# Graph layer on gathered columns: list tiles for 32-row groups, multiplied on column tiles, in place of early projection of the last rows

## The chip, the core and the metric

The kernel runs on one core of a Trainium2 chip. A core has five engines that run side by side and meet at semaphores: TensorE (PE, matmuls, with weight loads shown apart as PEld), VectorE (DVE), ScalarE (ACT), GpSimd (POOL) and SyncE (SP, which here only issues transfers). SBUF is its working memory, PSUM holds matmul results in banks, and 16 DMA engines carry data between SBUF and the memory outside (DRAM). The metric is the device time of the program in microseconds (us); lower is better.

## The reference

With x of 8 x 4096 x 256, adj of 4096 x 4096 and W of 256 x 256, all float32:

```python
HW = jnp.einsum('bnf,fo->bno', H, W)
A_norm = jax.nn.relu((A + A.T) * 0.5)
D = jnp.sum(A_norm, axis=1)
d_inv_sqrt = jnp.where(D > 0, D_safe ** (-0.5), 0.0)
DAD = d_inv_sqrt[:, None] * A_norm * d_inv_sqrt[None, :]
L_norm = jnp.eye(N) - DAD
out = jax.nn.relu(jnp.einsum('nm,bmo->bno', L_norm, HW))
result = layernorm(x + out)     # over the last axis
```

adj is sparse: 0.42% of the symmetrised matrix is not zero, and the entries are denser at low row and column numbers. The matrix is one for all eight batches, so one row of `g` (x W scaled by r, for all batches) has 8 x 256 = 2048 numbers, 8 KB.

## The kernel before, in words

The 4096 rows form 32 blocks of 128 (`NB`), and stage 1 walks squares of 512 rows (`NS` = 8 squares a side, `A` = 4 blocks each).

**Stage 1** (L191 to L308). For each pair of squares (i, j) with j >= i both adj squares are loaded (1 MB each, on SP's queue). `symmetrise` (L207) transposes on PE, adds on DVE (L215), halves and clips on ACT (L216), sums stretches of 128 columns into `part` (L217, DVE) and stores the result to `a_dram` from ACT's queue. When a row of squares is complete, `degrees` (L227) forms the degrees `e` and, with a power on POOL, `r`. `form(m, known)` (L238) projects block m: load of x (1 MB, SP), 16 transposes, 64 issued matmuls with W, then a copy on ACT and a store to `g_dram`. Where r of the block is known, ACT scales by it in the copy (L266). The last eight blocks (`HOLD`) are projected in the first row of squares, when no r is known: they are kept in SBUF (`held`), and `release` (L274) scales and stores them after the last degree. A `credit` of one projection for each pair of squares spreads the work.

**Lists.** A block of rows i needs only the columns in which one of its 128 rows has an entry. `places(s)` (L106) turns `part` into a mask for four blocks, and with two matmuls and a scan on DVE gives each used column a place; `make_list(i)` (L146) turns places into lists of row numbers: `hot` (L149) and three smaller comparisons and products on DVE, then 32 short matmuls (L169). A list tile holds 128 places. `CAP` fixes how many tiles a block has: 29 for the first, 9 for the last, 390 in all. Places that no column uses point to a row of zeros (row N of `a_dram` and `g_dram`).

**Stage 2** (L347 to L395). For each list tile POOL issues two indirect transfers: 128 pieces of 512 bytes of the symmetrised matrix (`ga`, L358), and 128 rows of g (`gg`, L365, 1 MB), each into one of ten buffers. PE multiplies them into four PSUM banks of 512 columns (L384); an f32 matmul is issued twice, so a tile is 8 matmuls. When all tiles of a block are in, `finish` (L311) subtracts from e times the block's own g (`gself`, loaded on SP's queue), applies r and relu on ACT, adds x and normalises on DVE, with a power on POOL (L334), and stores the output from ACT's queue.

The order on each engine is not the text's: a planner orders instructions by priority and readiness and sets the semaphores. If a block's list overflowed, a flag would start a full product (L403), which is not run with these inputs.

Of the kernel before, what the change touches and what calls it, by code (L numbers as in the profile page):

```python
# [8 lines left out]
F32 = mybir.dt.float32  # L9
# [7 lines left out]
CAP = [29, 21, 18, 17, 16, 15, 14, 13, 13, 13, 12, 12, 12, 11, 11, 11, 11] + [10] * 6 + [9] * 9  # L17
# [3 lines left out]
def kernel(  # L21
# [21 lines left out]
    nc = tc.nc  # L43
# [9 lines left out]
    HOLD = 8  # L53
    EPS = 1e-5

# [8 lines left out]
    part = const.tile([P, NB, NB], F32, name="part")  # L64
# [15 lines left out]
    lists = {}  # L80
    tmax = max(CAP)
# [19 lines left out]
    carry = const.tile([P, A, NB], F32, name="carry")  # L101
    nc.vector.memset(carry, 1.0)
    nc.vector.memset(carry[:, :, 0:1], 0.0)
    over = const.tile([P, NB], F32, name="over")

    def places(s):  # L106

        mask = ipool.tile([P, A, NB], BF16, tag="mask", name=f"mask_{s}")
        nc.vector.tensor_scalar(
            mask, part[:, :, s * A : (s + 1) * A].rearrange("p m i -> p i m"), 0.0, None, ALU.is_gt  # L110
        )
        pc = psum.tile([P, 2, A * NB], F32, tag="ix", name=f"count_{s}", bufs=2)
        mflat = mask.rearrange("p i m -> p (i m)")
        nc.tensor.matmul(pc[:, 0, :], lhsT=lower, rhs=mflat, start=True, stop=True)
        nc.tensor.matmul(pc[:, 1, :], lhsT=ones, rhs=mflat, start=True, stop=True)
        incl = ipool.tile([P, A * NB], F32, tag="incl", name=f"incl_{s}")
        nc.vector.tensor_tensor_scan(
            incl, carry.rearrange("p i m -> p (i m)"), pc[:, 1, :], 0.0, ALU.mult, ALU.add
        )
        for k in range(A):  # L120
            i = s * A + k
            nc.vector.tensor_scalar(
                over[:, i : i + 1],
                incl[:, (k + 1) * NB - 1 : (k + 1) * NB],
                float(CAP[i] * P),
                None,
                ALU.is_gt,
            )
        pos = ipool.tile([P, A * NB], F32, tag="pos", name=f"pos_{s}")
        nc.vector.tensor_sub(pos, incl, pc[:, 1, :])  # L130
        nc.vector.tensor_add(pos, pos, pc[:, 0, :])
        ip = ipool.tile([P, A * NB], I32, tag="ip", name=f"ip_{s}")
        nc.vector.tensor_copy(ip, pos)
        quot = ipool.tile([P, A * NB], I32, tag="quot", name=f"quot_{s}")
        nc.vector.tensor_single_scalar(quot, ip, 7, ALU.arith_shift_right)
        rem = ipool.tile([P, A * NB], I32, tag="rem", name=f"rem_{s}")
        nc.vector.tensor_single_scalar(rem, ip, P - 1, ALU.bitwise_and)

        at = ipool.tile([P, 2, A, NB], F32, tag="at", name=f"at_{s}")
        aq = at[:, 0].rearrange("p i m -> p (i m)")  # L140
        nc.vector.scalar_tensor_tensor(aq, quot, 1.0, mflat, ALU.add, ALU.mult)
        nc.vector.tensor_scalar(aq, aq, -1.0, None, ALU.add)
        nc.vector.tensor_copy(at[:, 1].rearrange("p i m -> p (i m)"), rem)
        return at

    def make_list(i, at):  # L146
        k, t = i % A, CAP[i]
        hot = ipool.tile([P, NB, P], BF16, tag="hot", name=f"hot_{i}")
# [13 lines left out]
        val = ipool.tile([P, NB, 2, tmax], BF16, tag="val", name=f"val_{i}")  # L162
# [28 lines left out]
    with (  # L191
        tc.tile_pool(name="adj", bufs=4) as apool,
        tc.tile_pool(name="hold", bufs=HOLD) as hpool,
# [13 lines left out]
        def symmetrise(i, j, tij, tji):  # L207
            sym = spool.tile([P, A, S], F32, tag="sym", name=f"sym_{i}_{j}")
            for a in range(A):
# [8 lines left out]
                part[:, i * A : (i + 1) * A, j * A : (j + 1) * A],  # L218
                sym.rearrange("p a (c q) -> p a c q", q=P),
# [16 lines left out]
        held = {}  # L236

        def form(m, known):  # L238

            xin = xpool.tile([P, B, F], F32, tag="xin", name=f"xin_{m}")  # L240
            nc.sync.dma_start(xin, x[:, m * P : (m + 1) * P, :].rearrange("b p f -> p b f"))
            xt = xpool.tile([P, B, FC, P], F32, tag="xt", name=f"xt_{m}", bufs=1)
# [6 lines left out]
            if known:  # L249
                g = xpool.tile([P, G], F32, tag="g", name=f"gt_{m}")  # L250
            else:
                g = hpool.tile([P, G], F32, tag="held", name=f"held_{m}")
            for b in range(0, B, 2):
# [10 lines left out]
                to = g[:, b * FO : (b + 2) * FO]  # L264
                if known:
                    nc.scalar.mul(to, pg, r[:, m : m + 1])  # L266
                else:
                    nc.scalar.copy(to, pg)
            if known:
                nc.scalar.dma_start(g_dram[m * P : (m + 1) * P, :], g)  # L270
            else:
                held[m] = g

        def release(m):  # L274
            g = held.pop(m)
            nc.scalar.mul(g, g, r[:, m : m + 1])
            nc.scalar.dma_start(g_dram[m * P : (m + 1) * P, :], g)


        known, early = [], list(range(NB - HOLD, NB))  # L280
        credit = 0.0
        for i in range(NS):
            for j in range(i, NS):
# [5 lines left out]
                credit += 1.0 if j > i else 0.5  # L289
                while credit >= 1.0 and (known or early):  # L290
                    if known:
                        form(known.pop(0), True)
                    else:
                        form(early.pop(0), False)
                    credit -= 1.0
# [161 lines left out]
```

## Time and profile before

| What | us |
|---|---|
| Median of three runs (1978.11 to 1985.22) | 1980.13 |
| The profiled execution's own time | 1980.13 |
| Its span, first to last instruction | 1978.2 |
| PE busy | 1819.9 |
| POOL busy | 918.9 |
| DVE busy | 887.4 |
| ACT busy | 348.1 |
| First `gg` gather starts at | 568.4 |
| Multiplication of list tiles on PE, from and to | 578.5 to 1957.8 |

Transfers moved 738 MB, 434.6 MB of it by POOL's gathers. In the profile's lines a group is: source line, engine, operation, output <- inputs, shape, count, then busy time in us and mean in ns, then the idle time of the engine just before these instructions and what ended it. In a listing in order of time, the two first numbers are start and length in us. In a list of stretches, each engine's busy time and instruction count follow the stretch, then the clock that TensorE was granted, the busy share of the DMA engines and GB/s. The chain of waits is what ended last, followed back.

### The profile page before, as it was taken

The numbers are of one execution on the slowest core, as the hardware profiler recorded it, in microseconds if no ns is written. First come the engines' busy times: TensorE is split into PE (matmuls) and PEld (weight loads), VectorE is DVE, ScalarE is ACT, GpSimd is POOL, SyncE is SP. The second block draws the span as 40 slices with busy tenths as digits, with TensorE's granted clock in tenths as the row PEclk, the third lists the DMA queues.
The fourth block names the chain that finished last, engine by engine and source line by source line (L and its number), as shares of the span: only waits on it lengthen the run. The fifth ranks groups of instructions, "written<-read, shape, count | busy, mean of one in ns | idle before, by whom it ended". The sixth has DMA issues, their size and how long they took to land.

```text
span 1978.2 us, 18260 instructions
## 1 busy us (share of the span) xinstructions
PE 1819.9 (92%) x6720; PEld 1006.8 (51%) x6720; DVE 887.4 (45%) x1679; ACT 348.1 (18%) x361; POOL 918.9 (46%) x830
## 2 busy tenths in 40 slices
PE   6988686879669999999999999999999999999995
PEld 5877575768544444444444444444444444444442
DVE  4778898755300102432226424523733733343334
ACT  3654443545620000000000000000000000000000
POOL 0000000000045655676558766865766865666662
PEclk8999897899889999999999999999999999999998
DMA  9998999999979999999998999899899999999994
GB/s 345 384 372 328 349 369 337 353 397 382 400 278 409 387 357 369 342 378 380 381 383 317 411 409 389 338 411 413 313 401 411 368 407 411 410 412 412 413 410 191
DMA packets 245726, 738.08 MB, mean 373 GB/s; under 512 B 17136, under 2 KB 115744, under 8 KB 187520
## 3 DMA queue, kind: packets, MB, share of 16 engines
q0 software_dynamic: 68640, 434.55, 55.3%
q1 hardware_dynamic: 104960, 167.78, 23.8%
q10 hardware_dynamic: 72032, 134.51, 17.7%
q8 instruction: 56, 0.92, 0.2%
q14 instruction: 38, 0.31, 0.0%
HBM read 602.54 MB, written 134.24 MB: 372 GB/s over the span
## 4 chain that ended last, share of the span: by engine, by line
PE 68%; DMA 13%; DVE 11%; issue 4%; ACT 3%; POOL 1%; SPq 0%; ACTq 0%; POOLq 0%; DVEq 0%
PE py L384 54%; PE pg L257 8%; DMA gg<-g_dram,gi 7%; PE tr L212 3%; DVE hot L149 3%; DMA a_dram<-sym 2%; DVE sym L215 2%; DMA adj<-in_adj_dram 2%; PE xtr L247 2%; DVE part L217 1%; ACT sym L216 1%; DMA xin<-in_x_dram 1%; PE pl L169 1%; DVE stats L331 1%; DVE y L326 1%
## 5 line engine op out<-in xcount | busy, mean ns | idle before, releaser
L384 PE MATMUL py<-gg,ga 128*128 128x512 f32 x3120 | 1363.6, 596 | 18.4 <-issue 16.0
L384 PEld LDWEIGHTS py<-gg,ga 128*128 128x128 f32 x3120 | 585.7, 190 | 726.6 <-issue 717.7
L358 POOL DMA_INDIRECT ga<-a_dram,ai x390 | 425.0, 1090 | 269.8 <-PE py L384 145.2
L365 POOL DMA_INDIRECT gg<-g_dram,gi x390 | 414.9, 1064 | 226.4 <-DMA gg<-g_dram,gi 109.7
L325 ACT ACTIVATE y<-y,r 128x2048 f32<-128x2048 f32 x32 | 64.1, 2002 | 1332.8 <-DVE y L317 1213.5
L257 PE MATMUL pg<-w_sb,xt 128*128 128x256 f32 x1024 | 247.6, 398 | 38.2 <-ACT xt L248 38.1
L317 DVE SCALAR_TENSOR_TENSOR y<-gself,e,py 128x512 f32<-128x512 f32 x128 | 95.1, 747 | 408.0 <-PE py L384 398.6
L234 POOL TENSOR_TENSOR r<-e,neg_half 128x4 f32<-128x4 f32 x8 | 8.1, 1011 | 510.3 <-DVE e L233 510.3
L257 PEld LDWEIGHTS pg<-w_sb,xt 128*128 128x128 f32 x1024 | 198.9, 199 | 76.3 <-ACT xt L248 48.5
L215 DVE TENSOR_TENSOR sym<-tr,adj 128x512 f32<-128x512 f32 x256 | 158.3, 683 | 115.4 <-PE tr L212 105.3
L212 PE MATMUL tr<-ident,adj 128*128 128x128 f32 x1024 | 132.1, 289 | 58.5 <-DVE sym L215 34.6
L185 DVE TENSOR_SCALAR ai<-low 128x9 uint32<-128x9 f32 (+11 forms) x32 | 6.5, 204 | 369.1 <-DMA ga<-a_dram,ai 369.1
L149 DVE TENSOR_TENSOR hot<-iota_q,at 128x4096 bf16<-128x4096 f32 x32 | 141.4, 4420 | 63.9 <-PE pl L169 48.9
L212 PEld LDWEIGHTS tr<-ident,adj 128*128 128x128 f32 x1024 | 123.7, 150 | 65.9 <-DVE sym L215 40.3
L217 DVE TENSOR_REDUCE part<-sym 128x16 f32<-128x2048 f32 x64 | 144.7, 2278 | 13.1 <-ACT sym L216 13.1
L216 ACT ACTIVATE sym<-sym 128x2048 f32<-128x2048 f32 x64 | 122.5, 1914 | 111.2 <-DVE sym L215 110.6
L336 DVE TENSOR_SCALAR y<-y,mv,rstd 128x256 f32<-128x256 f32 x256 | 87.2, 412 | 43.4 <-POOL rstd L334 43.4
L331 DVE BATCH_NORM_STATS2 stats<-y 128x6 f32<-128x256 f32 x256 | 99.3, 400 | 0.9
L326 DVE TENSOR_TENSOR y<-y,xr 128x2048 f32<-128x2048 f32 x32 | 73.4, 2293 | 56.0 <-ACT y L325 45.7
L334 POOL TENSOR_TENSOR rstd<-rstd,neg_half 128x8 f32<-128x8 f32 x32 | 69.5, 2173 | 42.2 <-DVE rstd L333 41.6
L248 ACT COPY xt<-xtr 128x512 f32<-128x512 f32 x128 | 69.8, 582 | 62.1 <-PE xtr L247 50.9
L247 PE MATMUL xtr<-ident,xin 128*128 128x128 f32 x512 | 72.5, 297 | 7.6 <-DVE sym L215 7.2
(50 smaller groups left out, 398.4 us busy)
## 6 DMA issues: line engine op xcount, KB each, us to landing
adj<-in_adj_dram SPq DMA_DIRECT2D x64, 1024.0 KB
a_dram<-sym ACTq DMA_DIRECT2D x64, 1024.0 KB
xin<-in_x_dram SPq DMA_DIRECT2D x32, 1024.0 KB
gself<-g_dram SPq DMA_DIRECT2D x32, 1024.0 KB
xr<-in_x_dram SPq DMA_DIRECT2D x32, 1024.0 KB
out_dram<-y ACTq DMA_DIRECT2D x32, 1024.0 KB
g_dram<-gt ACTq DMA_DIRECT2D x24, 1024.0 KB
g_dram<-held ACTq DMA_DIRECT2D x8, 1024.0 KB
```

Of the source, the lines that this page charges most:

```text
L149: nc.vector.tensor_tensor(hot, iota_q.unsqueeze(1).to_broadcast([P, NB, P]), at[:, 1, k, :].unsqueeze(2).to_broadcast([P, NB, P]), ALU.is_ ...
L212: nc.tensor.transpose(pt[:, c * P : (c + 1) * P], tji[:, c, a * P : (a + 1) * P], ident)
L215: nc.vector.tensor_add(sym[:, a, :], pt, tij[:, a, :])
L216: nc.scalar.activation(sym, sym, AF.Relu, scale=0.5)
L217: nc.vector.tensor_reduce(part[:, i * A : (i + 1) * A, j * A : (j + 1) * A], sym.rearrange("p a (c q) -> p a c q", q=P), AX.X, ALU.add,)
L247: nc.tensor.transpose(pt[:, k, c, :], xin[:, b + k, c * P : (c + 1) * P], ident)
L257: nc.tensor.matmul(pg[:, k * FO : (k + 1) * FO], lhsT=xt[:, b + k, c, :], rhs=w_sb[:, c, :], start=(c == 0), stop=(c == FC - 1),)
L317: nc.vector.scalar_tensor_tensor(yf[:, c * S : (c + 1) * S], gself[:, c * S : (c + 1) * S], e[:, i : i + 1], py[c], ALU.mult, ALU.subtract,)
L331: nc.vector.bn_stats(stats[:, b, :], y[:, b, :])
L358: nc.gpsimd.indirect_dma_start(out=at, out_offset=None, in_=a_rows, in_offset=bass.IndirectOffsetOnAxis(ap=ai[:, t : t + 1], axis=0),)
L365: nc.gpsimd.indirect_dma_start(out=gt, out_offset=None, in_=g_dram, in_offset=bass.IndirectOffsetOnAxis(ap=gi[:, t : t + 1], axis=0),)
L384: nc.tensor.matmul(py[c], lhsT=at, rhs=gt[:, c * S : (c + 1) * S], start=(t == 0), stop=(t == CAP[i] - 1),)
```

## The change

- **Two kinds of list tiles.** `part` now keeps sums of 32 columns. `places` finds, for each block, the columns used by exactly one of its four groups of 32 rows. Those get places in tiles of that group (`SINGLE` tiles for each group); all other columns, and what does not fit there, get places in common tiles (`MULTI`). That is 122 common tiles and 71 x 4 group tiles, 406 in all for 390.
- **Column tiles.** A common tile is multiplied as before. Four group tiles, one of each group, form a step: each is multiplied with only its 32 columns of `ga`, into 32 partitions of the same PSUM bank. So 122 + 71 = 193 steps take the place of 390.
- **Unused places are not fetched.** The `gg` gather has a bounds check and leaves out places that point to row N; the buffers (a ring of 14, `ga` 18) are cleared once.
- **Order of gathers.** In place of gathering block i + 1 after block i, after each step as many tiles are gathered as it used, 14 ahead.
- **Projection.** No block is projected early: `project` runs only after its r is known, the four blocks of a row of squares beside the next row, the last four after the first lists. `held`, `release` and the credit are gone. `adj` has five buffers for four, `xt` two for one.
- **`finish`** loads the block's own g into y itself in place of a tile `gself`. `hot` and `val` have one buffer for two.

```diff
-CAP = [29, 21, 18, 17, 16, 15, 14, 13, 13, 13, 12, 12, 12, 11, 11, 11, 11] + [10] * 6 + [9] * 9
+MULTI = [22, 9, 7, 6, 5, 4, 4, 5, 3, 4, 4, 4, 3, 3, 3, 3, 3] + [2] * 15
+SINGLE = [2, 3, 3, 3, 3, 3, 3, 2, 3, 2, 2, 2, 2, 2, 2, 2, 2] + [2] * 15
...
+    def prefix(mask, n, reset, name):
+        tot = psum.tile([P, n], F32, tag="ix", name=f"tot_{name}", bufs=2)
+        nc.tensor.matmul(tot, lhsT=ones, rhs=mask, start=True, stop=True)
+        low = psum.tile([P, n], F32, tag="ix", name=f"low_{name}", bufs=2)
+        nc.tensor.matmul(low, lhsT=lower, rhs=mask, start=True, stop=True)
+        incl = ipool.tile([P, n], F32, tag=f"incl{n}", name=f"incl_{name}", bufs=1)
+        nc.vector.tensor_tensor_scan(incl, reset, tot, 0.0, ALU.mult, ALU.add)
+        pos = ipool.tile([P, n], F32, tag=f"pos{n}", name=f"pos_{name}", bufs=1)
+        nc.vector.tensor_sub(pos, incl, tot)
+        nc.vector.tensor_add(pos, pos, low)
+        return pos, incl
...
+        cnt = ipool.tile([P, A, NB], F32, tag="cnt", name=f"cnt_{s}", bufs=1)
+        nc.vector.tensor_reduce(cnt, used.rearrange("p k c m -> p k m c"), AX.X, ALU.add)
+        one = ipool.tile([P, A, NB], BF16, tag="one", name=f"one_{s}", bufs=1)
+        nc.vector.tensor_scalar(one, cnt, 1.0, None, ALU.is_equal)
+        nc.vector.tensor_tensor(
+            used, used, one.unsqueeze(2).to_broadcast([P, A, K, NB]), ALU.mult
+        )
+        pos, _ = prefix(
+            used.rearrange("p k c m -> p (k c m)"),
+            A * K * NB,
+            carry.rearrange("p k c m -> p (k c m)"),
+            f"s{s}",
+        )
...
-        held = {}
-        def form(m, known):
+        def project(m):
...
-            if known:
-                nc.scalar.dma_start(g_dram[m * P : (m + 1) * P, :], g)
-            else:
-                held[m] = g
-        def release(m):
-            g = held.pop(m)
-            nc.scalar.mul(g, g, r[:, m : m + 1])
             nc.scalar.dma_start(g_dram[m * P : (m + 1) * P, :], g)
...
+                for _ in range(-(-len(todo) // (NS - j))):
+                    project(todo.pop(0))
             degrees(i)
+            todo += range(i * A, (i + 1) * A)
...
+        nc.sync.dma_start(yf, g_dram[i * P : (i + 1) * P, :])
         for c in range(G // S):
             nc.vector.scalar_tensor_tensor(
                 yf[:, c * S : (c + 1) * S],
-                gself[:, c * S : (c + 1) * S],
+                yf[:, c * S : (c + 1) * S],
...
+        ring = [gath.tile([P, G], F32, tag=f"g{k}", name=f"g{k}", bufs=1) for k in range(RING)]
+        for gt in ring:
+            nc.vector.memset(gt, 0.0)
...
+            gt = ring[n % RING]
+            nc.gpsimd.indirect_dma_start(
+                out=gt,
+                out_offset=None,
+                in_=g_dram,
+                in_offset=bass.IndirectOffsetOnAxis(ap=gi[:, t : t + 1], axis=0),
+                bounds_check=N - 1,
+                oob_is_err=False,
+            )
...
+                    for d, (at, gt) in enumerate(tiles):
+                        ds = slice(d * Q, (d + 1) * Q)
+                        nc.tensor.matmul(
+                            py[c][ds, :],
+                            lhsT=at[:, ds],
+                            rhs=gt[:, cols],
+                            start=first,
+                            stop=last,
+                            skip_group_check=True,
+                        )
+            for _ in ts:
+                gather(n)
+                n += 1
+            if last:
+                finish(i, py, ypool, stat)
```

## The prediction

> **What bounds the kernel now.** I read the page first for the stages. Its slices change at 562 us: ahead of it all engines work, behind it PE is full.
>
> ```profile
> PE   6988686879669999999999999999999999999995
> DMA  9998999999979999999998999899899999999994
> L384 PE MATMUL py<-gg,ga 128*128 128x512 f32 x3120 | 1363.6, 596 | 18.4 <-issue 16.0
> L358 POOL DMA_INDIRECT ga<-a_dram,ai x390 | 425.0, 1090 | 269.8 <-PE py L384 145.2
> L365 POOL DMA_INDIRECT gg<-g_dram,gi x390 | 414.9, 1064 | 226.4 <-DMA gg<-g_dram,gi 109.7
> ```
>
> PE and the DMA engines are both near full. Busy shares do not say which has room, so I cut the span in stretches (length, PE, PEld, DVE, ACT, POOL busy, clock, DMA share, GB/s):
>
> ```profile
> 0.00:519.00 519.00, 416.25 (x2720) 366.96 (x2721) 385.25 (x468) 255.96 (x296) 8.43 (x17) 0.92 0.98 363
> ...
> 1800.00:1900.00 100.00, 99.07 (x231) 43.38 (x231) 38.34 (x95) 8.01 (x4) 63.53 (x59) 1.00 1.03 412
> ```
>
> Stage 1 moves 363 GB/s with DMA at 0.98 and PE at 80%: transfers set its pace. Late in stage 2 the rate is 412 to 413 for 200 us; I take 413 GB/s as the ceiling. The chain there alternates between the two limits:
>
> ```profile
> 1652.25 55.05 PE py L384 x128
> ...
> 1731.57 13.90 DMA gg<-g_dram,gi
> 1745.73 14.47 DMA gg<-g_dram,gi
> ...
> 1905.84 51.96 PE py L384 x120
> ```
>
> From the first line, 128 matmuls in 55.05 us are 0.430 us each and 3.44 us for a list tile (8, since an f32 matmul is issued twice). 390 tiles are 1342 us of PE, plus some 37 us of list matmuls and gaps: PE works from 578.5 to 1957.8, 1379 us. The second and third show how close DMA is: a gather waits until the fourth one before it has landed (14 us), so only four tiles are in flight. Then POOL, in order of time:
>
> ```profile
> 1114.31 0.95 POOL L365 DMA_INDIRECT gg<-g_dram,gi  x1 [0.30 <-issue]
> 1115.56 0.96 POOL L358 DMA_INDIRECT ga<-a_dram,ai  x1 [0.30 <-DMA ga<-a_dram,ai]
> 1116.83 0.95 POOL L365 DMA_INDIRECT gg<-g_dram,gi  x1 [0.30 <-issue]
> ...
> 1227.28 4.72 POOL L365 DMA_INDIRECT gg<-g_dram,gi  x1 [0.31 <-issue]
> 1232.15 5.85 POOL L334 TENSOR_TENSOR rstd<-rstd,neg_half 128x8 f32<-128x8 f32 x1
> ```
>
> Unhindered, a tile costs POOL 2.51 us (two gathers of 0.95 and two gaps of 0.30). At 1227 a gather took five times as long: DVE worked on `hot` just then:
>
> ```profile
> 1226.80 4.39 DVE L149 TENSOR_TENSOR hot<-iota_q,at 128x4096 bf16<-128x4096 f32 x1
> ```
>
> **What the Trainium skill says.** (1) "TensorE: Matmul & The Clock Gate", Part 3, Measured speedup vs the span model: three column tiles at N=512 gave 2.38 times. No run here shows one. (2) "TensorEngine Tiling (Array Packing)", Key Properties: changing the tiling mode drains TensorE; that is two changes a block, nothing against 33 us. (3) "SBUF — State Buffer", Who interferes with whom: a DVE instruction with two SBUF inputs contends with a GpSimd instruction that reads SBUF. The trace agrees: 4.72 for 0.95 us. (4) "DMA: Bandwidth & Descriptors", The descriptor swizzle: in a transfer over 128 partitions, the DMA engine follows from the partition, engines 0 to 7 writing partitions 0 to 63. The trace does not name engines.
>
> **The change, part by part.** Counted from the reference's inputs, 45,244 (block, column) rows are used. No region overflows (the tightest has 379 of 384 places), so the full path stays off.
>
> PE. Of 406 tiles 122 stay full: 122 x 3.44 = 420 us. The other 284 go in 71 steps of four. If the four do not overlap a step is 4 x 3.44 = 13.8 us; if they overlap fully, 3.44. Each f32 matmul is two passes of one column tile[...] I expect the second pass of one beside the first of the next: half of 13.8, 6.9 us. 71 x 6.9 = 490. PE then needs 910 us for 1342 and has room whatever lies between 3.44 and about 12 us. With gaps PE is granted less clock: 0.78 in the stretch 562 to 600, where it waits for gathers. 910/0.78 is 1167, still below DMA.
>
> DMA. All bytes together fall: 45,244 x 8 KB = 371 MB for 409, and 16 tiles more add 1 MB. But places fill from partition 0 and the unused ones are the last of a region, so they sit in the upper partitions. If engines follow partitions, the busiest engine fetches 3,115 rows; before, each had 390 x 8 = 3,120. Its bytes are 25.5 MB of g, 1.7 of a, and 6.3 of the block's own g, x and output (32 x 3 x 65,536): 33.5 MB at 413/16 = 25.8 GB/s, 1297 us, for 1296 before. The saving in bytes buys no time. If engines shared the rest, it would be 1206 us; I take 1297.
>
> POOL. 406 x 2.51 = 1019 us. `pow` 32 x (1.67 + 0.19) = 60. Each list locks POOL for `hot` and the three short operations, 5.4 us, of which some 0.6 is gap anyway: 26 lists lie in stage 2, 26 x 4.8 = 125. The residual add (2.29 us) costs some 1.7: 32 x 1.7 = 54. `places` grows from 128 to 512 elements, from about 3 to 12 us by DVE's rows of 128 elements (0.22 to 0.42); six lie in stage 2, perhaps 3 us each against POOL: 18. Sum 1276. On DVE itself the 9 us more each are covered, since it is busy 39% late in stage 2; so is the wait for list matmuls that a single `hot` and `val` buffer brings (the next list on DVE waits for PE's 32 short ones, 2 to 3 us). Uncovered, they are 54 and 26 x 3 = 78 us. A bounds check on a gather has no row: below, it may save up to 13% of 0.95 us where rows are skipped (-0.1), above, I bound it by half a gather (+0.5). I take 0.
>
> So DMA (1297) and POOL (1276) bind together, with only four tiles between them. A lock of 5 us is covered as long as the four tiles in flight (11 us) last; POOL wins back 3.2 - 2.5 us a tile. Before, with POOL at 80% of the DMA time, five late blocks took 161.6 us for 159.5 of transfers, 1.3% over. With POOL at 98% I expect a third of its lock time to show: (125 + 54) x a quarter to a third, 45 us; between 0 and 179. Sum 1342 us. The ring of 14 and the 18 `ga` buffers cost and bring nothing, since four in flight is the limit.
>
> Stage 1. Up to the last degree 24 projections lie beside the symmetrised blocks: 134.2 MB + 24 x 2.1 = 184.5 MB at 363 GB/s, 508 us. Then eight projections in PE's order, 8.66 us from one to the next (544.96 to 553.62): 577 us, for 562 before: +15. It is +4 if the four known ones are pulled ahead, +40 if the first row without projections leaves DMA idle. The eight scalings of held tiles (2 us each on ACT) go. The 14 memsets of the ring (2.3 us each at most, by the 2048-element add) lie on DVE beside the last projections, where it is idle (0.00 busy at 562 to 600); uncovered, they cost 32 us. An extra `adj` and `xt` buffer I cost at nothing, as transfers set the pace.
>
> `finish`. g now lands in y itself, so its load waits for the output of two blocks before (two y buffers). On SP nothing but the next x row queues behind it. Pow to output to load is about 6 + 10 + 11 us, and two blocks are 66: hidden; if not, DVE's subtraction, PE's banks and then the gathers are late.
>
> Sum: first g gather 568.4 + 15 = 583; 1342 to the last landing; 5 us of latency and 5 for the last step on PE; 21 from PE's end to the span's end, as before (1957.2 to 1978.2). 1956, and 2 us around the span as in the profiled execution (1980.13, which is also the median): **1958 us**, 1% faster.
>
> **Rivals.**
> - *Bytes saved count in full.* If engines share the load, DMA needs 1206 and POOL's 1276 binds, with 25 us of coupling: 583 + 1301 + 31 + 2 = 1917 us. For it: 38 MB less. Against it: the skill's partition rule.
> - *POOL becomes the bound, slower than before.* One mechanism: the bounds-checked gather costs more on POOL. With +0.35 us, 1276 + 142 = 1418 us; 583 + 1418 + 31 + 2 = 2034. It ends slower than before from about +0.22 us (406 x 0.22 = 89, and 583 + 1276 + 89 + 33 = 1981). For it: POOL has no room left, and every g gather carries the check; against it: no row shows a check, and skipped rows leave less to issue.
> - *The column tiles do not overlap.* PE needs 420 + 71 x 13.8 + 37 = 1437 us from 593 on: 593 + 1437 + 21 = 2051; with weight loads exposed (284 x 8 x 0.05 to 0.19 us) up to 2200. It decides from 12.9 us a step. For it: nothing in the trace shows overlap; against it: the skill's 2.38.
> - *The transfers were hidden anyway* is the forecast itself: PE halves and time hardly moves.
>
> **How the numbers follow.** Forecast 45% (own range 1930 to 1995: coupling 0 to 80 us, stage 1 +4 to +30); full saving 12%; dearer POOL 23%; no overlap 20%. Under 1900 lie some 4%, above 2070 some 14%. Within 0.5% (1970 to 1990), what a measurement here can tell from no change, falls a quarter of the forecast and a little of the POOL case, 14%; faster 42% (29 + 12 + 1), slower 44%.
>
> **What would show it.** The spacing of a column step: 6.9 us right, 13.8 wrong. PE idle for some 40% of stage 2, waiting for gg. GB/s lower, near 385, at a DMA share still near 1. POOL's median gather still 0.95, its waits for landings short. First g gather near 583. Wrong would be: a stage 2 at 413 GB/s (bytes do count), gathers of 1.2 us, or a stage 1 past 610.

## The result, and the profile after

The changed kernel takes 2031.84 us (median of four, 2027.29 to 2039.49) where the kernel before takes 1982.68: 1.0251 times as long, interval 1.0204 to 1.0298. The forecast was 1958 and faster, with an own range of 1930 to 1995; the time lies above that range, on the other side of no change. The profiled execution has a span of 2033.9 us.

First the page of the changed kernel: busy tenths in 40 slices of 51 us, then the groups that answer to those shown of before (busy us, mean ns, idle time just before and what ended it).

```profile
PE   4586878889978999979769989776768866557554
DMA  9999899999759999999997999998999998898892
L445 PE MATMUL py<-g,ga 128*128 128x512 f32 x976 | 493.9, 660 | 162.5 <-DVE y L350 131.9
L451 PE MATMUL py<-g,ga 128*32 128x512 f32 x2272 | 554.6, 599 | 17.4 <-issue 12.3
L416 POOL DMA_INDIRECT g<-g_dram,gi x406 | 474.4, 1168 | 192.5 <-issue 106.9
L407 POOL DMA_INDIRECT ga<-a_dram,ai x406 | 437.8, 1078 | 188.7 <-issue 110.7
```

PE is no longer full behind slice 12, as forecast, and it empties towards the end (5, 5, 7, 5, 5, 4). But the first line of matmuls waited 131.9 us for `y L350`, the subtraction in `finish`. That is not a wait for gathers, and the forecast's sum has nothing for it. And DMA has its lowest slices (7, 5), the last one apart, at 510 to 610 us, at the end of stage 1. So I took two stretches (length, PE, PEld, DVE, ACT, POOL busy, clock, DMA share, GB/s). After the change:

```profile
500.00:600.00 100.00, 96.50 (x547) 86.11 (x545) 16.07 (x21) 54.91 (x86) 2.02 (x2) 1.00 0.68 232
...
1700.00:1800.00 100.00, 61.30 (x230) 20.78 (x225) 30.48 (x83) 6.00 (x3) 62.48 (x59) 0.80 0.89 328
```

And before the change:

```profile
500.00:600.00 100.00, 68.81 (x284) 50.74 (x285) 10.00 (x13) 42.18 (x50) 26.09 (x27) 0.85 0.87 339
```

At 500 to 600 us the changed kernel is bound by PE (96.5) on projections while DMA is at 0.68; the kernel before is already in stage 2 for the last 30 us of it. At 1700 to 1800 us nothing is full: PE 61, POOL 62, DMA 0.89 at 328 GB/s, where before it was 413. Something serial holds them all. The list of waits (total, times, longest, in us) names it:

```profile
DVE y L350 <- DMA y<-g_dram: 332.1, 18, 33.6
...
POOL rstd L367 <- DVE rstd L366: 139.4, 11, 24.1
PE py L445 <- DVE y L350: 131.9, 8, 25.2
```

DVE's subtraction waits for the load of the block's own g into y, PE waits for the subtraction (it frees PSUM banks), and POOL waits in its power for DVE's statistics. (The chain of waits of this page is of no use: it breaks off 22 us before the end, at the last subtraction.) How late the load is, and why, is read from the listing in order of time over two blocks, of which only the lines that matter stand here (SPq and ACTq are instructions that issue a transfer from that engine's queue):

```profile
1689.61 2.72 DVE L350 SCALAR_TENSOR_TENSOR y<-y,e,py 128x512 f32<-128x512 f32 x4 [33.18 <-DMA y<-g_dram]
1700.17 2.67 DVE L369 TENSOR_SCALAR y<-y,mv,rstd 128x256 f32<-128x256 f32 x8
1700.41 1.82 POOL L367 TENSOR_TENSOR rstd<-rstd,neg_half 128x8 f32<-128x8 f32 x1 [15.20 <-DVE rstd L366]
1702.93 0.38 ACTq L377 DMA_DIRECT2D out_dram<-y  x1
1709.01 0.34 SPq L348 DMA_DIRECT2D y<-g_dram  x1
1718.31 2.72 DVE L350 SCALAR_TENSOR_TENSOR y<-y,e,py 128x512 f32<-128x512 f32 x4 [15.31 <-DMA y<-g_dram]
1728.86 2.68 DVE L369 TENSOR_SCALAR y<-y,mv,rstd 128x256 f32<-128x256 f32 x8
1731.63 0.38 ACTq L377 DMA_DIRECT2D out_dram<-y  x1
1755.29 0.34 SPq L348 DMA_DIRECT2D y<-g_dram  x1
1764.72 2.72 DVE L350 SCALAR_TENSOR_TENSOR y<-y,e,py 128x512 f32<-128x512 f32 x4 [32.99 <-DMA y<-g_dram]
```

This is a loop. Call the block of the first line k. The normalisation 10.6 us after it (L369) is not block k's: by the order of instructions it is that of block k-1, which the planner put behind block k's statistics. Then comes the output of k-1, and only when it has landed may y of block k+1 be loaded into the same buffer (6.1 us after the issue the first time, 23.7 us the second; in SP's own list of waits, these loads stand behind the output in 24 waits, 612 us in all). 9.3 us later the load has landed, and the subtraction of block k+1 starts. So one block, not two, goes round the loop at a time: 28.7 us, then 46.4 us, and so on in turn, 37.5 us a block where before it was 30.9. The quick landing falls just behind a pause of POOL (it had waited 15.2 us for its power, and sent its next gather only at 1702.30), the slow one amid gathers.

In the kernel before, the listing of DVE has the other order: subtraction (L317), the end of the statistics (L333), the normalisation (L336), and only then the subtraction of the next block:

```profile
1128.92 2.05 DVE L317 SCALAR_TENSOR_TENSOR y<-gself,e,py 128x512 f32<-128x512 f32 x3
1138.73 0.17 DVE L333 TENSOR_SCALAR rstd<-mv 128x8 f32<-128x8 f32 x1
1152.20 2.67 DVE L336 TENSOR_SCALAR y<-y,mv,rstd 128x256 f32<-128x256 f32 x8
1173.31 0.75 DVE L317 SCALAR_TENSOR_TENSOR y<-gself,e,py 128x512 f32<-128x512 f32 x1 [17.88 <-PE py L384]
```

By the order of instructions it is so in all 32 blocks before. In the changed kernel the normalisation is late for the first time in the seventh block, and from the twelfth block to the thirtieth it always stands behind the next block's statistics.

### The profile page after: what moved, and what is told of

The parts are those of the page before. It is cut to its first block, busy times and chain, and to the rows that moved or that the text cites. A ratio compares the mean times of both kernels' runs of the same rounds, so it can differ in the third digit from the quotient of the medians.

```text
span 2033.9 us, 19384 instructions
## 1 busy us (share of the span) xinstructions
PE 1529.4 (75%) x6862; PEld 785.6 (39%) x6864; DVE 982.5 (48%) x1853; ACT 337.0 (17%) x353; POOL 983.3 (48%) x1054
## 5 line engine op out<-in xcount | busy, mean ns | idle before, releaser
L445 PE MATMUL py<-g,ga 128*128 128x512 f32 x976 | 493.9, 660 | 162.5 <-DVE y L350 131.9
L451 PE MATMUL py<-g,ga 128*32 128x512 f32 x2272 | 554.6, 599 | 17.4 <-issue 12.3
L416 POOL DMA_INDIRECT g<-g_dram,gi x406 | 474.4, 1168 | 192.5 <-issue 106.9
L445 PEld LDWEIGHTS py<-g,ga 128*128 128x128 f32 x976 | 200.8, 212 | 460.3 <-issue 307.6
L350 DVE SCALAR_TENSOR_TENSOR y<-y,e,py 128x512 f32<-128x512 f32 x128 | 88.4, 744 | 482.5 <-DMA y<-g_dram 332.1
L451 PEld LDWEIGHTS py<-g,ga 128*32 128x32 f32 x2272 | 151.7, 110 | 398.0 <-issue 394.0
L209 DVE TENSOR_TENSOR hot<-iota_q,at 128x4096 bf16<-128x4096 f32 x32 | 141.5, 4421 | 66.0 <-PE pl L229 23.7
L276 DVE TENSOR_REDUCE part<-sym 128x64 f32<-128x2048 f32 x64 | 144.7, 2277 | 6.9 <-ACT sym L275 6.8
L229 PE MATMUL pl<-val,hot 128*128 128x20 bf16 (+10 forms) x1024 | 40.6, 175 | 114.0 <-DVE low L239 57.6
L369 DVE TENSOR_SCALAR y<-y,mv,rstd 128x256 f32<-128x256 f32 x256 | 86.1, 409 | 44.9 <-POOL rstd L367 44.9
L317 ACT ACTIVATE gt<-pg,r 128x512 f32<-128x512 f32 x128 | 87.9, 690 | 112.3 <-PE pg L310 110.2
L229 PEld LDWEIGHTS <-hot 128*128 128x128 bf16 x1024 | 38.3, 97 | 160.3 <-issue 141.4
```

Of the source, the lines that this page charges most:

```text
L209: nc.vector.tensor_tensor(hot, iota_q.unsqueeze(1).to_broadcast([P, NB, P]), at[:, 1, k, :].unsqueeze(2).to_broadcast([P, NB, P]), ALU.is_ ...
L276: nc.vector.tensor_reduce(part[:, i * A : (i + 1) * A, j * S // Q : (j + 1) * S // Q], sym.rearrange("p a (c q) -> p a c q", q=Q), AX.X, A ...
L317: nc.scalar.mul(g[:, b * FO : (b + 2) * FO], pg, r[:, m : m + 1])
L350: nc.vector.scalar_tensor_tensor(yf[:, c * S : (c + 1) * S], yf[:, c * S : (c + 1) * S], e[:, i : i + 1], py[c], ALU.mult, ALU.subtract,)
L416: nc.gpsimd.indirect_dma_start(out=gt, out_offset=None, in_=g_dram, in_offset=bass.IndirectOffsetOnAxis(ap=gi[:, t : t + 1], axis=0), boun ...
L445: nc.tensor.matmul(py[c], lhsT=at, rhs=gt[:, cols], start=first, stop=last, skip_group_check=True)
```

## The experiments

Each row is against the kernel before on the same chip. "First g" is the start of the first gather of g in us, from the profiled run.

| Run | Median, us | Ratio to before (interval) | First g |
|---|---|---|---|
| the change | 2031.84 | 1.0251 (1.0204 to 1.0298) | 611.1 |
| own_g_tile | 1969.24 | 0.9928 (0.9901 to 0.9955) | 603.3 |
| ring_12 | 1976.20 | 0.9982 (0.9966 to 0.9998) | 601.8 |
| early_proj | 1998.38 | 1.0080 (1.0059 to 1.0100) | 573.7 |
| own_g_early | 1937.85 | 0.9771 (0.9748 to 0.9794) | 578.2 |
| rstd_act | 1927.90 | 0.9726 (0.9696 to 0.9756) | 606.0 |
| rstd_act_late | 2062.87 | 1.0432 (1.0403 to 1.0460) | 603.5 |
| y_three | 1942.96 | 0.9817 (0.9799 to 0.9834) | 607.0 |
| rstd_act_12 | 1943.60 | 0.9810 (0.9776 to 0.9845) | 602.4 |
| before_rstd | 1972.97 | 0.9962 (0.9948 to 0.9976) | 571.1 |
| base2 | 1898.48 | 0.9573 (0.9545 to 0.9601) | 573.0 |
| base2_full | 2031.17 | 1.0251 (1.0228 to 1.0274) | 573.3 |
| base2_all | 1950.42 | 0.9838 (0.9807 to 0.9869) | 574.0 |
| base2_halves | 1888.69 | 0.9522 (0.9494 to 0.9550) | 580.4 |
| base2_even | 1894.77 | 0.9561 (0.9536 to 0.9585) | 574.6 |

**An own tile for g (own_g_tile), and its control (ring_12).** The tile of before comes back; the ring shrinks by two to make room, and the control shrinks the ring alone.

```diff
-    RING = 14
+    RING = 12
...
+        gself = ypool.tile([P, G], F32, tag="gself", name=f"gself_{i}")
+        nc.sync.dma_start(gself, g_dram[i * P : (i + 1) * P, :])
-        nc.sync.dma_start(yf, g_dram[i * P : (i + 1) * P, :])
...
-                yf[:, c * S : (c + 1) * S],
+                gself[:, c * S : (c + 1) * S],
```

> The changed kernel, but g of the block lands in a tile of its own again (two buffers, loaded ahead of x, as before the change); the ring shrinks from 14 to 12 to make room. Theory 'y loop' (output of block k-1 must land before the y load of block k+1 starts, so that one block at a time goes round subtraction, stats, output, load): the waits of DVE for y vanish, the late blocks fall from 28/46 us in turn to 32 us or less, stage 2 (first g gather to the end of the span) falls from 1423 us by 50 to 80 us, total 1950 to 1985. Rival 'POOL or column steps set stage 2': the wait only moves to g or ga, total within 10 us of the changed kernel, 2020 to 2042. Rival 'transfers set it, with one engine as full as before': a gain of under 15 us.

> The changed kernel with 12 g buffers instead of 14 and nothing else: the control for the kernel with an own g tile. Theory 'y loop': only four tiles are in flight, so two buffers less cost nothing while DVE is on time, but where PE is held up the ring lets POOL run ahead by two tiles less: 2030 to 2045. Rival 'the ring is what matters': more than 15 us either way.

The first gained 63 us, as expected, but the control gained 56 where 15 were the most expected (9 of the 56 are an earlier first gather). My theory fell in the form it had: the tile is not what mattered. The control's listing of DVE, ACT and SP shows what did:

```profile
1679.16 2.72 DVE L350 SCALAR_TENSOR_TENSOR y<-y,e,py 128x512 f32<-128x512 f32 x4 [8.18 <-DMA y<-g_dram]
1683.95 2.29 DVE L359 TENSOR_TENSOR y<-y,xr 128x2048 f32<-128x2048 f32 x1 [1.79 <-ACT y L358]
1686.16 2.67 DVE L369 TENSOR_SCALAR y<-y,mv,rstd 128x256 f32<-128x256 f32 x8
1688.92 0.38 ACTq L377 DMA_DIRECT2D out_dram<-y  x1
1692.10 0.19 DVE L366 TENSOR_SCALAR rstd<-mv 128x8 f32<-128x8 f32 x1
1712.61 0.34 SPq L348 DMA_DIRECT2D y<-g_dram  x1
```

The normalisation of the block before (L369) now stands behind block k's residual add and ahead of its statistics (which end at L366). The output leaves 9.8 us after the start of the subtraction, in the changed kernel 13.3. The ring's length changed the planner's order on DVE, and the loop became shorter. It did not go: DVE's waits for the load of y are 233.5 us in sum here, for 332.1 in the changed kernel. With the own tile as well, the load is out of the loop but the output is not: the subtraction writes y, which the output of two blocks before must have left. Its list of waits says so:

```profile
DVE y L351 <- DMA out_dram<-y: 136.8, 13, 20.8
```

So the new theory is: the order of the normalisation, and with it the cycle of the two y buffers, costs the time.

**The early projections of before (early_proj, own_g_early).** `project` is replaced by the `form`, `release` and credit of before, with seven held tiles instead of eight, four `adj` buffers and one `xt`:

```diff
-        def project(m):
+        def form(m, known):
...
-                for _ in range(-(-len(todo) // (NS - j))):
-                    project(todo.pop(0))
+                credit += 1.0 if j > i else 0.5
+                while credit >= 1.0 and (known or early):
```

own_g_early has this and the own tile with its ring of 12.

> The changed kernel with the stage 1 of before (projections of the last rows formed early, held in seven tiles, scaled when their degrees are known; four adj buffers). Theory 'late projections cost 40 us': first g gather from 611 us back to 570 to 580, total 1990 to 2005. Rival 'stage 1 only lays bare what stage 2 hides' (the start of stage 2 then waits for lists instead): less than half of it, 2012 to 2030.

> Both edits at once: own g tile (ring of 12) and the early projections of before. If both theories hold the gains add: first g gather at 570 to 580, stage 2 of 1345 to 1375 us, total 1920 to 1950, faster than before. If POOL, the column steps or the transfers set stage 2: 1985 to 2005.

The first g gather moves from 611.1 to 573.7 us and the total falls by 33: stage 1 cost what was expected, and stage 2 did not take it back. With the own tile the gains add up (63 + 33; measured 94).

**The order restored (rstd_act, base2).** The power leaves POOL; with it the planner puts each block's normalisation directly behind its own statistics.

```diff
-        nc.gpsimd.tensor_tensor(rstd, rstd, neg_half[:, :B], ALU.pow)
+        nc.scalar.sqrt(rstd, rstd)
+        nc.vector.reciprocal(rstd, rstd)
```

base2 has this and the early projections.

> The changed kernel (ring of 14, g in y itself, late projections) with one edit: the power that gives rstd leaves POOL; ACT takes a square root and DVE a reciprocal. With it DVE's order becomes subtraction, stats, normalisation of one and the same block, where the changed kernel normalises block k-1 only after block k's stats. Theory 'order of the normalisation' (the ring of 14 costs 55 us over 12 only because it moves the normalisation of block k-1 behind the stats of block k, which leaves the y load one block instead of two): DVE's waits for y fall below 60 us in sum, the late blocks go from 28/46 us in turn to 33 to 34 us, total 1945 to 1975 with stage 1 unchanged (first g gather at 605 to 615). Rival 'g in y itself is too slow whatever the order': waits for y stay over 200 us, total over 2000. Rival 'more gathers in flight with a longer ring': no change, 2020 to 2040.

> The same edit and the early projections of before as well: ring of 14, g in y itself, column tiles, skipped places. If stage 1 and the order of the normalisation are all that cost time: first g gather at 570 to 580, total 1910 to 1940. If POOL (power taken off it, some 60 us) was the limit with the own g tile: 1900 or less. If transfers of the fullest engine limit it (1297 us estimated from the first gather on): not under 1905.

rstd_act is 104 us faster than the change, more than expected. base2, which also projects early, is at 1898 us, below its expected band too: inside the band set for POOL (1900 or less), and 7 us under the 1905 that the transfers were to allow. So base2 by itself does not tell those two limits apart. The listing of DVE, SP and ACT of rstd_act:

```profile
1677.61 3.32 DVE L350 SCALAR_TENSOR_TENSOR y<-y,e,py 128x512 f32<-128x512 f32 x4 [0.89 <-PE py L452]
1682.02 0.34 SPq L348 DMA_DIRECT2D y<-g_dram  x1
1689.37 2.67 DVE L370 TENSOR_SCALAR y<-y,mv,rstd 128x256 f32<-128x256 f32 x8
1692.13 0.38 ACTq L378 DMA_DIRECT2D out_dram<-y  x1
1711.39 3.32 DVE L350 SCALAR_TENSOR_TENSOR y<-y,e,py 128x512 f32<-128x512 f32 x4 [0.94 <-PE py L452]
1714.16 0.34 SPq L348 DMA_DIRECT2D y<-g_dram  x1
```

The subtraction now waits for PE, not for y. The load that starts at 1682.02 is for the subtraction at 1711.39, so it has 29 us and needs some 9. Its blocks take 33.8 us.

**Order or power? (rstd_act_late, y_three)** rstd_act changed both. So one run keeps the power off POOL and brings the late order back, by making the normalisation of block k-1 depend on block k's variance; the other keeps POOL's power and the late order, and breaks the cycle with a third y buffer (ring of 13 to make room).

```diff
# rstd_act_late: normalise(mv of block k) is called after the stats of block k
+            nc.vector.scalar_tensor_tensor(
+                rstd, after[:, :, 1], 0.0, rstd, ALU.mult, ALU.add
+            )
# y_three
-    RING = 14
+    RING = 13
-        y = ypool.tile([P, B, FO], F32, tag="y", name=f"y_{i}")
+        y = ypool.tile([P, B, FO], F32, tag="y", name=f"y_{i}", bufs=3)
```

> As rstd_act (square root on ACT, no power on POOL, ring of 14), but the normalisation of block k-1 is tied behind the stats of block k, as the changed kernel has it: one short DVE operation adds zero times the variance of block k to rstd of block k-1. Theory 'order of the normalisation': the loss comes back, DVE's waits for y over 250 us, late blocks alternating or over 36 us, total 2000 to 2040. Rival 'rstd_act gained by taking the power off POOL': within 15 us of rstd_act, 1915 to 1945.

> The changed kernel with three y buffers (ring of 13 to make room), power still on POOL, normalisation still behind the stats of the next block. Theory 'the y buffer cycle': the y load of block k+1 then waits for the output of block k-2, DVE's waits for y fall below 60 us, late blocks 33 to 35 us, total 1935 to 1975 with stage 1 unchanged. Rival 'POOL's wait at the power for the stats sets the pace': total over 2000.

Both came out for the order. rstd_act_late loses 135 us against rstd_act (at 2063 us it is above the 2040 that I had expected at most), with this wait in its list:

```profile
DVE y L350 <- DMA y<-g_dram: 466.1, 21, 31.5
```

It is slower even than the change, presumably because there the order is late only from the seventh block on (by the order of instructions), here from the first. y_three gains 89 us over the change, and its subtraction waits for PE again:

```profile
DVE y L350 <- PE py L451: 141.5, 30, 19.6
```

Its ring of 13 shifts DVE's order a little as well: the normalisation stands behind the next block's statistics only from the seventeenth block on. From there to the last block both kernels have the same late order, and the subtractions span 551 us in the changed kernel, 501 with the third buffer. These 50 us are the buffer cycle alone; the other 39 may in part be the order.

**Controls of the same edit (before_rstd, rstd_act_12).** The square root on ACT in the kernel before, and rstd_act with a ring of 12.

```diff
# before_rstd, in the kernel before
-        nc.gpsimd.tensor_tensor(rstd, rstd, neg_half[:, :B], ALU.pow)
+        nc.scalar.sqrt(rstd, rstd)
+        nc.vector.reciprocal(rstd, rstd)
# rstd_act_12, on rstd_act
-    RING = 14
+    RING = 12
```

> The kernel before with the square root on ACT and the reciprocal on DVE in place of the power on POOL, nothing else. PE sets its stage 2 and its normalisation already follows its own block: 1970 to 1985, within 0.5% of before. Rival 'taking the power off POOL is worth 50 us by itself, whatever the order': 1940 or less.

> As rstd_act (the changed kernel with the square root on ACT), with the ring of 12 in place of 14. Theory 'the ring's length mattered only through DVE's order': within 10 us of rstd_act, 1918 to 1938. Rival 'a shorter ring is faster in itself': 1890 or less.

Before, the edit is worth 0.4%: its normalisation was not late. With the order mended, the ring of 12 is 16 us slower than the ring of 14, a little outside what I expected, and DVE's order of subtraction, statistics and normalisation is the same in both. So the longer ring helps by itself; in the changed kernel, where the shorter one gained 56 us, it hurt by way of DVE's order.

**Column tiles undone (base2_full).** On top of base2, the four tiles of a step are multiplied at full width, one after another.

```diff
-                            py[c][ds, :],
-                            lhsT=at[:, ds],
...
+                        py[c],
+                        lhsT=at,
...
+                        start=first and d == 0,
+                        stop=last and d == len(tiles) - 1,
```

> As base2, but the list tiles of one group are multiplied at full width, one after another, like the others (the unused columns are zeros, the sum is the same): only the column tiles are undone. Theory 'column tiles free PE': PE needs 406 x 3.44 = 1397 us and some 40 us of list products and gaps from 584 us on, total 2030 to 2055. Rival 'PE was not the limit' (transfers at 413 GB/s all along): under 1960.

133 us slower than base2, inside the expected band, and PE is full in every stretch from 700 to 1850 us, as in this one:

```profile
1000.00:1100.00 100.00, 100.00 (x275) 44.59 (x274) 41.83 (x106) 4.42 (x4) 60.52 (x58) 1.00 0.90 330
```

**Which rows the DMA engines fetch (base2_all, base2_halves, base2_even).** All on base2: without the bounds check; with halves of places swapped in every second pair of tiles; with places dealt over all engines.

```diff
# base2_all
-                bounds_check=N - 1,
-                oob_is_err=False,
# base2_halves, in places()
+        nc.vector.tensor_single_scalar(half, ip, 2, ALU.arith_shift_right)
+        nc.vector.tensor_single_scalar(half, half, P // 2, ALU.bitwise_and)
+        nc.vector.tensor_tensor(ip, ip, half, ALU.bitwise_xor)
# base2_even: iota_e holds the numbers 0 to 127 in permuted order, in make_list()
-            iota_q.unsqueeze(1).to_broadcast([P, NB, P]),
+            iota_e.unsqueeze(1).to_broadcast([P, NB, P]),
```

> As base2, without the bounds check: unused places fetch the row of zeros, 6,724 more rows of 8 KB (55 MB). Theory 'the fullest engine sets the time': the fullest engine then fetches 3,248 rows instead of 3,115, 42 us more if nothing else gives, GB/s of late stage 2 back at 410; POOL's gather 0.95 us instead of 1.00: total 20 to 45 us over base2. Rival 'all bytes count' (55 MB at 413 GB/s): 130 us more. Rival 'POOL sets the time': equal or less than base2.

> As base2, but in every second pair of list tiles the two halves of 64 places are swapped (bit 6 of a place is flipped by bit 8 of the place number), so that unused places lie in lower and upper partitions alike. The same rows are fetched. By the partition rule the fullest DMA engine then fetches 2,948 rows instead of 3,115. Theory 'the fullest engine sets the time': 167 rows of 8 KB at 25.8 GB/s an engine are 53 us; some of it meets POOL: 30 to 55 us less than base2, GB/s of late stage 2 from about 370 to 385 or more. Rival 'engines share the rows, or POOL sets the time': within 8 us of base2.

> As base2, but the 128 places of a list tile are dealt out over the partitions so that any first n of them spread evenly over the 16 DMA engines of the partition rule (a permuted row of numbers in the comparison that makes the list; no instruction more in stage 2). The fullest engine then fetches 2,884 rows in place of 3,115, and each partly filled tile is spread over all engines. Theory 'the fullest engine of each tile sets the transfer time': 231 rows are 73 us on that engine; since POOL's gathers and the first block (PE) then limit parts of stage 2, as they did when the halves were swapped (10 us of 53), 15 to 45 us less than base2, late blocks from 32.8 us to 31 us or less. Rival 'engines share rows freely': within 6 us of base2.

In sum the expectations were missed more than met. Fetching all costs 52 us: above the 20 to 45 expected with the fullest engine (42 estimated for that engine alone), far below the 130 of all bytes. The two even placements gain only 10 and 4 us where 30 and 15 were the least expected; the 4 lie in the band of the rival that engines share rows freely, the 10 just past that of its rival. The late blocks, where the lists are nearly done and POOL has room, speak for the fullest engine all the same. From base2, base2_all, base2_halves and base2_even, in this order:

```profile
1600.00:1850.00 250.00, 231.07 (x606) 65.78 (x606) 85.94 (x229) 16.66 (x15) 154.32 (x152) 1.00 0.98 370
```

```profile
1600.00:1850.00 250.00, 229.35 (x584) 62.05 (x583) 84.56 (x229) 15.47 (x14) 146.88 (x144) 1.00 1.03 413
```

```profile
1600.00:1850.00 250.00, 231.47 (x636) 67.88 (x633) 92.17 (x245) 17.48 (x15) 164.99 (x160) 1.00 1.01 386
```

```profile
1600.00:1850.00 250.00, 231.37 (x645) 66.96 (x645) 95.06 (x260) 17.68 (x16) 168.77 (x163) 1.00 1.02 397
```

| Run | Rows of the fullest engine in a late block | Estimate, us | Measured, us |
|---|---|---|---|
| base2_all | 80.0 | 34.6 | 34.5 |
| base2 | 75.3 | 33.1 | 32.8 |
| base2_halves | 70.6 | 31.6 | 31.5 |
| base2_even | 66.6 | 30.4 | 30.7 |

The rows are counted from the inputs by the partition rule, the mean of the last ten blocks. The estimate is rows x 8192 bytes + 10 x 4096 (ga) + 3 x 65,536 (own g, x, output), over the prediction's 25.8 GB/s an engine; measured is the distance of the subtractions on DVE over ten late blocks. base2, base2_halves and base2_even fetch exactly the same rows, so a limit by bytes alone would give them one time. The Trainium skill's rule ("DMA: Bandwidth & Descriptors", The descriptor swizzle), which puts partitions 0 to 63 on engines 0 to 7, agrees with all four within 0.4 us. The last of the ten distances is short in every run, since no gathers follow it; over the ten before it the measured means are 34.7, 33.2, 31.7 and 31.3, in the same order and within 0.7 us of the estimates for those blocks. The mean share of the DMA engines does not show it: it is 0.98 in base2, at 370 GB/s. The trace does not name engines, so the runs show that the placement over partitions counts; that it is the engine, and not something else that goes with the partition, is the rule's word.

Why the middle blocks gave nothing of this back is argued, not shown: POOL is nearly full in some stretches. base2_halves, for one of them:

```profile
800.00:900.00 100.00, 91.43 (x333) 30.35 (x332) 47.11 (x111) 2.70 (x4) 77.76 (x67) 1.00 0.99 382
```

67 gaps of 0.30 us beside the 77.76 are 98 of 100 us, but the same count gives only some 88 at 700 to 800 and at 1100 to 1200 us. In base2_even the ten blocks after the first were even 42 us slower than in base2; what holds them stays open, and that profiled execution is the slowest of its four runs.

Over the whole of stage 2 (from the first gather of g for the first block to that for the last, the estimates summed block by block as in the table) base2 takes 1261 us for an estimate of 1265 and base2_all 1311 for 1305, but base2_halves 1250 for 1231 and base2_even 1272 for 1194. So the fullest engine accounts for base2 and base2_all; once it has less to fetch, something else sets the pace of the middle blocks.

## Why the prediction was wrong

**The step that failed: `finish`.** "Pow to output to load is about 6 + 10 + 11 us, and two blocks are 66: hidden". The load was costed at nothing. Three things were wrong in it. The output does not follow from pow alone but from the normalisation, which waits in DVE's order: from the twelfth block on it stood behind the *next* block's subtraction and statistics, so the time to hide in was one block, not two. The landing of the output was taken as 10 us; amid gathers it took 23.7. From subtraction to output, landing and load, 13.3 + 23.7 + 9.4 us then stood against one block. And the sum takes the order for granted that DVE has in the kernel before; with the change the planner chose another. The ring of 14 has a part in that, since ring_12 moves the normalisation forward again and gains 56 us. The prediction had put that ring at nothing ("cost and bring nothing, since four in flight is the limit"). What else in the change moves the planner is not shown. The sentence after it was right: "if not, DVE's subtraction, PE's banks and then the gathers are late" is what the waits show. Its price is 89 us by y_three, which also has a ring of 13, and 104 us by rstd_act, which also takes POOL's power away.

**Stage 1: direction right, size off.** The forecast was +15 with bounds of +4 and +40; the first g gather came 42.7 us later (568.4 to 611.1), just past the upper bound and past the 610 that the prediction had named as a sign of being wrong. The bytes' share, 508 us to the last degree, was too short: the power for it came at 534.25 us. Up to then 191 MB had passed, not 184.5 (358 GB/s at a DMA share of 0.97), so it seems that some of what the forecast put behind the last degree came ahead of it; in the first 100 us PE was only 47.5% busy, for 80.9% before, and PE leads at the end (the stretch at 500 to 600 us: DMA 0.68). That the projections crowd into the later rows is in the code; how much each of these adds is not measured. Then seven projections follow at the 8.66 us that the forecast used. early_proj gives 37.4 us of the start and 33 us of the time back.

The memsets did not lie beside the last projections, as the forecast had it. DVE waits for the last projection's store to land (70.1 us) and then clears the 14 buffers of g (the 18 of `ga` are not cleared) from 604.3 to 633.9 us, beside the first gathers. What that costs no run shows.

**PE: right.** A column step was put at 6.9 us. Where all gathers are in, the listing of PE in the changed kernel has 64 matmuls of L451, two steps, in 12.38 us, 6.2 us each:

```profile
1690.41 7.63 PE L445 MATMUL py<-g,ga 128*128 128x512 f32 x12 [16.40 <-DVE y L350]
1697.97 12.38 PE L451 MATMUL py<-g,ga 128*32 128x512 f32 x64
```

That is 2.2 times faster than four tiles one after another (13.8 us); the three column tiles of the Trainium skill ("TensorE: Matmul & The Clock Gate", Part 3, Measured speedup vs the span model) gave 2.38, so four gain less here than three there. In this stretch the starts come in twos at first and later in threes, 0.43 us apart, so the half of the forecast is near the size but not the whole pattern. The change between the two kinds of matmul, put at nothing, leaves no gap in the listing. The rival without overlap is refuted (its upper end is also added wrongly: 284 x 8 x 0.19 us are 432, which would make 2483, not 2200), and base2_full shows what the column tiles are worth once nothing else is in the way: 133 us.

**DMA: right for base2, but it could not show at first.** The forecast had 1297 us from the first gather to the last landing and 10 more to the last step on PE: in base2 1304 us pass from the first g gather (573.0) to the last multiplication (1877.1). The rival that counts all bytes would have had 1206. The late blocks agree with the fullest engine. Another limit lies close behind it, as the even placements show: 53 and 73 us less for that engine brought 10 and 4. In the changed kernel all this was hidden under the loop.

**POOL: nearly right.** The bounds check costs 0.054 us a gather (median 0.990 us with it in base2, 0.936 without it in base2_all), 22 us over 406 gathers. The rival of a dearer gather needed 0.22 us each to end slower than before. At 0.35 us it gave 2034, near the measured time, with a mechanism that did not occur: POOL's listing of the changed kernel has gathers of 0.96 and 1.01 us, and the means of its two groups, DVE's hindrance included, sum to 2.25 us a tile for 2.15 before.

**Coupling: too dear, it seems.** 45 us were set for DMA and POOL meeting. Where the loop is broken and POOL's power kept, y_three needs 1334 us from its first g gather (607.0) to the end of the span (1941.4); the forecast's way of counting gives 1342 + 31 = 1373. So some 40 us of the forecast's stage 2 were not there. That they belong to this term, and not to POOL's or DMA's, is not shown.

Put together by these terms: 1958 + 28 (stage 1 over the forecast) + 89 (the y cycle) - 40 (the rest) = 2035, for 2031.84 measured. The 40 and the 89 both come from y_three, so the sum closes by construction and proves no term. The column tiles and skipped places without the two losses, with the early projections back and the power off POOL, are base2: 1898 us, against 1973 for the kernel before with the same power edit. base2_halves, at 1889 us, is the fastest kernel of this study, 4.8% faster than before. Its interval overlaps base2's at the edge (0.9494 to 0.9550, 0.9545 to 0.9601), but its four runs on the same chip (at most 1892.12) all lie below base2's (at least 1894.84).

## What to carry to other kernels

When a change lets a load land in a buffer that was written, worked on and stored before, count the whole cycle of that buffer (every operation and transfer from the first write to the store's landing) with the order that the planner really gave each engine, and with the landing time beside the traffic of that stage. A third buffer, or a shorter way to the store, is the cheap insurance; changing another pool's depth can reorder an engine that has nothing to do with it, so a control for such a side change is worth its run. Where rows are left out of transfers, count them by the engine that fetches the most, not by the sum, and look for the limit that comes next.

## What the runs showed of the hardware that I had not expected

- The landing of a 1 MB output took 6.1 us just behind a pause of POOL and 23.7 us amid gathers (issue to the load that waits for it, in the changed kernel); a 1 MB load of g beside gathers took 9.3 us.
- Three placements of the same rows give late blocks of 32.8, 31.5 and 30.7 us, while the mean share of the DMA engines is 0.98 to 1.02.
- In the stretches in which PE waited more, the clock granted to it was lower: 0.80 at 1700 to 1800 us of the changed kernel (PE busy 61%), 1.00 in base2 in the same stretch (92%); 0.75 in the first 100 us of the changed kernel (48%), 0.95 in the kernel before (81%).
